# The gate's logits of a mixture-of-experts layer, taken from eight extra columns of the attention's output projection

## The chip, the cores and the metric

The kernel runs on one core of one Trainium2 chip. The metric is device time in microseconds for one execution of the whole kernel; smaller is better. Of several runs the median is given.

## The reference

The input `x` is 2 x 56 x 56 x 256 in fp32. The reference runs two layers over it. Layer 0 is group norm and a 7 x 7 neighbourhood attention with 8 heads, added to `x`. Layer 1 works on the 2 x 3136 tokens of 256 values: a causal linear attention with gates and cumulative sums, and then a feed-forward part with 8 experts of hidden size 512, of which each token takes the two with the largest gate probability. Cut to layer 1:

```
t = t + attn(ln(t), wq, wk, wv, wo, ...)      # ends in  ctxt @ wo.T + bo
z = ln(t)                                     # (t - mean) / sqrt(var + 1e-5)
logits = z @ gate_w + gate_b                  # gate_w: 256 x 8
probs  = softmax(logits)
cw     = probs where among the token's top 2, else 0
t = t + sum over experts e of cw[:, e] * (gelu(z @ W1[e] + b1[e]) @ W2[e] + b2[e])
```

The LayerNorm `z` is needed twice: as the experts' input and for the gate's logits.

## The kernel before, in words

Layer 0 takes the first 447 us and is the same in both kernels. Layer 1 goes over the tokens in 14 steps. A step is 224 tokens of each of the two batch entries, 448 in all, held as four tiles of 112 tokens (`NTI` = 4, `TT` = 112). Three generators and the experts' work make up a step:

- `before_pairs(s)` loads the tokens into `x_acc`, normalizes them to `xn`, transposes `xn` on TensorE (`pt_x`, copied by ScalarE to `xT_a`), and makes q, k, v (`p_qkv`), an auxiliary product (`p_u`), the sums over each head (`p_sum`, from products `pd`) and the scans over the tokens that yield the gate factor `gl` and the coefficients `cf`. It also adds the output bias `bo` to `x_acc`.
- `attention(s)` makes the cumulative sums in pairs of blocks (`p_gt`, `kt`, `vt`, `sc`, `qv`, the running state `zz`, `z` and `zc`, outputs `po`) and then the output projection `p_out`, which is added to `x_acc`.
- `route(s)` stores `x_acc` to the output, normalizes it to `xs`, transposes `xs` (again `pt_x`, copied to `xT_f`), multiplies with the gate's weights (`p_gate`), and goes on with softmax (`pb`), the rank of each expert (`rank`, `taken`), two small matmuls that count tokens by expert (`p_n`), slot numbers (`slot`, `rowi`), and eight indirect DMAs on GpSimd's queue that scatter the rows of `xs` to `xs_d` in DRAM, sorted by expert. `listed` then keeps the list of expert tiles.
- `experts()` goes through 56 tiles of 256 slots. For each it fetches the rows (`xg`) and the expert's weights (`wj`, 1.15 MB) on SP's queue, takes the token numbers out of `xg` (`rows_e`), transposes (`pt_g`), multiplies twice (`p_h`, `hT`, `p_y`), scales (`ye`) and adds the result to the output by an indirect DMA on GpSimd's queue (`out<-ye`).

Both normalizations are one function, `norm_T`: statistics of four tiles (`lst`, `lmv`), standard deviation by a square root on ScalarE (`lrs`), its reciprocal, four `tensor_scalar` operations on VectorE, eight transposes and two copies.

The function `together` interleaves the generators in step s: `attention(s)` leads, with it run `route(s - 1)`, `before_pairs(s + 1)` and expert tiles, each at a given share of the leader's yields (`n_step, n_route = 45, 13`). So the tokens of step s - 1 are normalized for the routing while those of step s + 1 are normalized for the attention. Below that a scheduler sets the final order of the instructions on each engine by its priorities and its own estimates of costs. An engine runs its instructions in that order. The matmuls of all these parts take their PSUM tiles from one pool of six (`l_mm`).

Expert tiles start in step 4, as tokens must have been routed first. After the last step the route of step 13 stands alone with four expert tiles; then follow some sixteen expert tiles until the end.

Layer 1 exists twice in the program, a plain form and a general one, and a value `plain`, worked out from the inputs in layer 0, decides by a branch which one runs. Here it is the plain one.

Of the kernel before, what the change touches and what calls it, by code (L numbers as in the profile page):

```python
# [14 lines left out]
F32 = mybir.dt.float32  # L15
I32 = mybir.dt.int32
U32 = mybir.dt.uint32
AF = mybir.ActivationFunctionType
ALU = mybir.AluOpType
AX = mybir.AxisListType  # L20
PSUM = bass.MemoryType.PSUM
DRAM = bass.MemoryType.DRAM

P = 128
NB = 2
IMG = 56
L = IMG * IMG
C = 256
NG = 2
# [11 lines left out]
TT = 112  # L41
BLK = 448
BT = BLK // NB
NST = L // BT
NTI = BLK // TT
CH = 8
NCH = TT // CH
NE, FF = 8, 512
NF = FF // P
GN_EPS = 1e-5  # L50
LN_EPS = 1e-5
# [6 lines left out]
NX = (2 * NB * L - NE) // SL + NE  # L58
TOK, CWC = C, C + 1
ROW = C + 16  # L60


def sure(s):
# [90 lines left out]
def hybrid_kernel(ctx: ExitStack, tc: tile.TileContext, t: dict, out: bass.AP):  # L154
    nc = tc.nc
    const = ctx.enter_context(tc.tile_pool(name="const", bufs=1))
# [4 lines left out]
    x1_d = dram.tile([NB, IMG, IMG, C], F32, name="x1_d")  # L161
    xs_d = dram.tile([NE * RG + SL, ROW], F32, name="xs_d")
    ident = const.tile([P, P], F32, name="ident")
# [13 lines left out]
    def load(pool, name, shape, src, eng=None, dt=F32):  # L177
        dst = pool.tile(shape, dt, name=name)
        (eng or nc.sync).dma_start(out=dst, in_=src)
        return dst  # L180

    def load_wT(pool, name):
        return load(pool, name, [P, NG, C], t[name].rearrange("(k p) o -> p k o", p=P))


    wq1, wk1, wv1, wo1 = (load_wT(const, f"L1_w{n}T") for n in "qkvo")
    bq1, bk1, bv1 = (load(const, f"b{n}1", [P, NG], t[f"L1_b{n}P"]) for n in "qkv")
    bo1 = load(
        const, "bo1", [TT, C], t["L1_attn_wo_b"].unsqueeze(0).to_broadcast([TT, C])
# [65 lines left out]
    with tc.tile_pool(name="once", bufs=1) as once:  # L255
        s_all = once.tile([P, NG, HD], F32, name="s_all")
        for h in range(4):
            nc.sync.dma_start(
                out=s_all[h * HD : (h + 1) * HD],
                in_=s_row.rearrange("(g h) e -> h g e", g=NG)[h]  # L260
                .unsqueeze(0)
                .to_broadcast([HD, NG, HD]),
            )
        nc.vector.tensor_tensor(s_all, s_all, s_sb, ALU.is_equal)
        nc.vector.tensor_reduce(same, s_all, AX.XY, ALU.min)
    plain = const.tile([1, 1], I32, name="plain")
    ones = const.tile([NB * NH, BT], F32, name="ones")
    nc.gpsimd.memset(ones, 1.0)
# [66 lines left out]
    with (  # L335
# [250 lines left out]
        nc.vector.tensor_reduce(mx[:, 1:2], pf[:, NG + 1, :], AX.X, ALU.min)  # L586
        nc.vector.tensor_copy(plain, mx[:, 1:2])

    flag = nc.values_load(
# [56 lines left out]
    def layer_1(general):  # L648
        with (
# [48 lines left out]
                nc.gpsimd.memset(qh, 0.0)  # L698
                qhs.append(qh)

            def norm_T(x, tag, pool, xn=None):

                st = p2.tile([TT, NTI, 6], F32, tag="lst", name="lst")
                mv = p2.tile([TT, NTI, 2], F32, tag="lmv", name="lmv")
                for i in range(NTI):
                    nc.vector.bn_stats(st[:, i, :], x[:, i, :])  # L706
                    nc.vector.bn_aggr(mv[:, i, :], st[:, i, :])
                rs = p2.tile([TT, NTI], F32, tag="lrs", name="lrs")
                nc.vector.tensor_scalar_add(rs, mv[:, :, 1], LN_EPS)
                nc.scalar.activation(rs, rs, AF.Sqrt)  # L710
                nc.vector.reciprocal(rs, rs)
                xT = pool.tile([P, NG, BLK], F32, tag=tag, name=tag)
                if xn is None:
                    xn = p1.tile([TT, NTI, C], F32, tag="xn", name="xn")
                yield
                for i in range(NTI):
                    nc.vector.tensor_scalar(
                        xn[:, i, :C],
                        x[:, i, :],
                        mv[:, i, 0:1],  # L720
                        rs[:, i : i + 1],
                        ALU.subtract,
                        ALU.mult,
                    )
                for g in range(NG):
                    pt = ps_m.tile([P, NTI, TT], F32, tag="mm", name="pt_x")
                    for i in range(NTI):
                        nc.tensor.transpose(  # L728
                            pt[:, i, :], xn[:, i, g * P : (g + 1) * P], ident[:TT, :TT]
                        )  # L730
                    nc.scalar.copy(xT[:, g, :], pt.rearrange("p i t -> p (i t)"))
                    yield
                return xT

            def before_pairs(s):

                nonlocal m_prev, s_prev, g_prev
                x = p4.tile([TT, NTI, C], F32, tag="x", name="x_acc")
                for b in range(NB):
                    nc.sync.dma_start(  # L740
                        out=x[:, b * 2 : (b + 1) * 2, :],
                        in_=x1_d[b]
                        .rearrange("r c e -> (r c) e")[s * BT : (s + 1) * BT]
                        .rearrange("(i p) e -> p i e", p=TT),
                    )
                yield
                xT = yield from norm_T(x, "xT_a", p1)
                nc.vector.tensor_tensor(
                    x, x, bo1.unsqueeze(1).to_broadcast([TT, NTI, C]), ALU.add
                )  # L750
                q, k, v = (
                    p2.tile([P, NG, BLK], F32, tag=n, name=n) for n in ("q", "k", "v")
# [38 lines left out]
                for g in range(NG):  # L791
                    for b in range(NB):
                        for n in range(4):
                            nc.tensor.matmul(
                                ps[n * HD : n * HD + NHB, :],
                                lhsT=ind[:, g, b, :],
                                rhs=pd[:, n, g, b * BT : (b + 1) * BT],
                                start=at == 0,
                                stop=at == NB * NG - 1,
                            )  # L800
                        at += 1
                row = [NHB, BT]

                def part(n):
# [12 lines left out]
                gl = p2.tile(row, F32, tag="gl", name="gl")  # L817
                nc.vector.tensor_tensor(gl, part(3), rk, ALU.mult)
                yield


                m = p2.tile([NHB, BT + 1], F32, tag="m", name="m")
# [155 lines left out]
            def attention(s):  # L978
                x, q, k, v, gl, cf = ready.pop(s)
                yield from (sums_general if general else sums_plain)(s, q, k, v, gl, cf)  # L980

                for i in range(NTI):
                    ps = ps_m.tile([TT, C], F32, tag="mm", name="p_out")
                    for g in range(NG):
                        nc.tensor.matmul(  # L985
                            ps,
                            lhsT=q[:, g, i * TT : (i + 1) * TT],
                            rhs=wo1[:, g, :],
                            start=g == 0,
                            stop=g == NG - 1,  # L990
                        )
                    nc.vector.tensor_tensor(x[:, i, :], ps, x[:, i, :], ALU.add)
                    yield
                routed[s] = x
                if general:
                    yield from route(s)
# [160 lines left out]
            def route(s):  # L1157
# [3 lines left out]
                for b in range(NB):  # L1161
                    stored.append(
                        nc.gpsimd.dma_start(
                            out=out[b * L + s * BT : b * L + (s + 1) * BT].rearrange(
                                "(i p) e -> p i e", p=TT
                            ),
                            in_=x[:, b * 2 : (b + 1) * 2, :],
                        )
                    )
                xs = p3.tile([TT, NTI, ROW], F32, tag="xs", name="xs")  # L1170
                nc.gpsimd.memset(xs[:, :, CWC + NE :], 0.0)
                xT = yield from norm_T(x, "xT_f", p1, xs)
                pg = ps_m.tile([TT, NTI, NE], F32, tag="mm", name="p_gate")
                for i in range(NTI):
                    for k in range(NG):
                        nc.tensor.matmul(  # L1176
                            pg[:, i, :],
                            lhsT=xT[:, k, i * TT : (i + 1) * TT],
                            rhs=gw[:, k, :],
                            start=k == 0,  # L1180
                            stop=k == NG - 1,
                        )
                pb = p2.tile([TT, NTI, NE], F32, tag="pb", name="pb")
                red = p2.tile([TT, NTI], F32, tag="red", name="red")
                nc.vector.tensor_tensor(
                    pb, pg, gb.unsqueeze(1).to_broadcast([TT, NTI, NE]), ALU.add
                )
                nc.vector.tensor_reduce(red, pb, AX.X, ALU.max)
                nc.vector.tensor_tensor(
                    pb, pb, red.unsqueeze(2).to_broadcast([TT, NTI, NE]), ALU.subtract  # L1190
# [34 lines left out]

                taken = p2.tile([TT, NTI, NE], F32, tag="taken", name="taken")
                nc.vector.tensor_single_scalar(taken, rank, 1.5, ALU.is_lt)
                yield
                pn = ps_m.tile([P, 2, NTI, NE], F32, tag="mm", name="p_n")
                flat = taken.rearrange("p i e -> p (i e)")  # L1230
# [289 lines left out]
            tiles = experts()  # L1520
            per_tile = NF + 1 + SL // P
            n_before = sum(1 for _ in before_pairs(0)) + 1
            n_step, n_route = 45, 13
            for s in range(NST):
                n_tiles = max(0, sure(s - 1) - wait) - max(0, sure(s - 2) - wait)
                begin = n_tiles and sure(s - 2) <= wait
# [92 lines left out]
```

## Time and profile before

| | us |
|---|---|
| median of 3 runs | 1600.95 (1599.42 to 1603.63) |
| the profiled execution, its own time | 1586.77 |
| its span | 1584.9 |
| layer 0, to `plain` | 0 to 447 |
| between the layers, to the first matmul of layer 1 | 447 to 462.6 |
| steps of layer 1 | 463 to 1388 |
| last routing, to the last scatter's issue | 1388 to 1417 |
| last expert tiles | 1417 to 1584.9 |

The span runs from the first to the last instruction. Over it TensorE was busy 1379.4 us (87%), VectorE 921.9 (58%), ScalarE 707.0 (45%) and GpSimd 449.5 (28%), and the mean granted TensorE clock was 0.935. PE is TensorE's matmul, PEld its weight loads, DVE is VectorE, ACT ScalarE, POOL GpSimd, SP SyncE. A fp32 matmul appears as two records in the profile. Durations are taken from the one profiled execution.

### The profile page before, as it was taken

How to read it: one execution, taken by the hardware profiler on the slowest of the kernel's cores; microseconds unless marked ns; L12 is line 12 of the kernel's file. 1: busy time of each engine (PE TensorE's matmuls, PEld its weight loads, DVE VectorE, ACT ScalarE, POOL GpSimd, SP SyncE). 2: the span in 40 equal slices, each digit the busy share in tenths (PEclk: the TensorE clock that was granted, in tenths of full speed). 3: DMA queues.
4: the chain of work that ended last, by engine and by line, in shares of the span. 5: the costliest groups of instructions: out<-in, count | busy, mean ns of one | idle time of the engine just before them, and what ended most of it. 6: DMA issues, size and time to landing. Idle time of an engine off the chain costs nothing. (4 is left out here: it accounts for less than half of the span.)

```text
span 1584.9 us, 28462 instructions
## 1 busy us (share of the span) xinstructions
PE 1379.4 (87%) x10672; PEld 1008.6 (64%) x10672; DVE 921.9 (58%) x2731; ACT 707.0 (45%) x1261; POOL 449.5 (28%) x496
## 2 busy tenths in 40 slices
PE   0789999999957779878999998999999899879996
PEld 0357667677834445555766766676776667667885
DVE  3546566656646786785756757576766757441221
ACT  0333343444424344335664655565555546243342
POOL 2113233333320021112233231313223232343443
PEclk9989999999969688679999999999999999889998
DMA  7445554455520010114434443434443443459884
GB/s 222 140 130 167 161 171 151 138 164 156 165 70 0 24 48 26 36 36 173 121 116 116 114 119 110 125 104 119 110 113 105 130 112 93 120 162 264 234 231 90
DMA packets 110769, 197.66 MB, mean 125 GB/s; under 512 B 17666, under 2 KB 92274, under 8 KB 103444
## 3 DMA queue, kind: packets, MB, share of 16 engines
q1 hardware_dynamic: 74596, 135.60, 26.8%
q0 software_dynamic: 32560, 54.55, 14.9%
q10 hardware_dynamic: 3456, 5.51, 1.1%
q8 instruction: 88, 1.44, 0.4%
q14 instruction: 69, 0.57, 0.1%
HBM read 138.85 MB, written 56.73 MB: 123 GB/s over the span
## 5 line engine op out<-in xcount | busy, mean ns | idle before, releaser
L1457 POOL DMA_INDIRECT out<-ye,rows_e x112 | 176.8, 1579 | 429.7 <-DVE ye L1454 199.4
L1409 PE MATMUL p_h<-xT_g,wj 128*128 128x256 f32 x896 | 233.8, 395 | 4.9 <-DVE ye L1454 4.9
L1447 PE MATMUL p_y<-wj,hT 128*128 128x256 f32 x896 | 217.0, 389 | 7.6 <-issue 4.0
L1409 PEld LDWEIGHTS p_h<-xT_g,wj 128*128 128x128 f32 x896 | 168.1, 196 | 47.9 <-issue 19.8
L1447 PEld LDWEIGHTS p_y<-wj,hT 128*128 128x128 f32 x896 | 169.9, 194 | 44.1 <-issue 18.2
L512 ACT ACTIVATE ex<-ex 98x1024 f32<-98x1024 f32 x98 | 103.9, 1060 | 202.5 <-DVE ex L506 193.5
L1267 POOL DMA_INDIRECT xs_d<-xs,rowi x112 | 106.7, 953 | 194.5 <-DVE pos L1322 73.8
L506 DVE TENSOR_TENSOR ex<-sc,bias 98x1024 f32<-98x1024 f32 x98 | 119.5, 1220 | 47.8 <-PE sc L497 42.5
L1416 ACT ACTIVATE hT<-p_h,wj 128x256 f32<-128x256 f32 x224 | 103.9, 471 | 87.7 <-PE p_h L1409 79.5
L521 PE MATMUL po<-vw,ex 98*64 98x33 f32 x3136 | 116.6, 227 | 8.3 <-DMA vw<-v_d 8.2
L1454 DVE SCALAR_TENSOR_TENSOR ye<-p_y,cws,ye 128x256 f32<-128x256 f32 x112 | 53.5, 478 | 116.1 <-PE p_y L1447 115.9
L521 PEld LDWEIGHTS po<-vw,ex 98*64 98x64 f32 x3136 | 104.5, 141 | 24.7 <-DMA vw<-v_d 10.1
L1441 ACT ACTIVATE ye<-wj,cws 128x256 f32<-128x256 f32 x112 | 54.4, 502 | 143.7 <-DVE own_e L1428 114.4
L497 PEld LDWEIGHTS sc<-qb,kc 64*98 64x98 f32 x1568 | 92.5, 166 | 40.6 <-issue 26.4
L497 PE MATMUL sc<-qb,kc 64*98 64x128 f32 x1568 | 114.4, 285 | 1.3 <-DVE ex L506 1.3
L926 PE MATMUL sc<-qh,v 128*112 128x448 f32 x224 | 109.4, 575 | 0.0
L934 DVE TENSOR_TENSOR qv<-sc,upto 112x448 f32<-112x448 f32 x112 | 68.9, 616 | 57.8 <-PE sc L926 55.9
L324 POOL TENSOR_TENSOR xo<-xo,xq 128x256 f32<-128x256 f32 x49 | 35.5, 725 | 157.6 <-DVE xo L318 149.0
L1424 DVE CAST rows_e<-xg 128x2 int32<-128x2 f32 x56 | 9.3, 166 | 116.6 <-DMA xg<-xs_d 116.5
L985 PE MATMUL p_out<-L_woT,q 128*112 128x256 f32 x224 | 64.3, 417 | 9.1 <-DVE q L975 9.1
L1416 ACT ACT_TABLE_LOAD x44 | 56.5, 1283 | 26.6 <-PE p_h L1409 26.0
L446 ACT ACTIVATE kc<-pk,bk 128x112 f32<-128x112 f32 x196 | 50.6, 371 | 37.4 <-PE pk L415 37.4
(229 smaller groups left out, 2468.2 us busy)
## 6 DMA issues: line engine op xcount, KB each, us to landing
wj<-in_we SPq DMA_DIRECT2D x56, 1154.0 KB
vw<-v_d SPq DMA_DIRECT2D x196, 101.1 KB
xg<-xs_d SPq DMA_DIRECT2D x56, 272.0 KB
v_d<-values POOLq DMA_DIRECT2D x28, 231.0 KB
xq<-in_x SPq DMA_DIRECT2D x98, 64.0 KB
q_d<-evq POOLq DMA_DIRECT2D x28, 224.0 KB
qb<-q_d SPq DMA_DIRECT2D x56, 112.0 KB
x_d<-xo POOLq DMA_DIRECT2D x98, 64.0 KB
```

Of the source, the lines that this page charges most:

```text
L497: nc.tensor.matmul(sc[:KN, p, b, k], lhsT=keys(i, j, k, b, rows, g), rhs=qb[rows, g, :, b, j * QN : (j + 1) * QN], start=True, stop=True,)
L506: nc.vector.tensor_tensor(ex[:KN], sc[:KN].rearrange("n p b k h q -> n p b (k h q)"), tables[kind][:KN, g].unsqueeze(2).to_broadcast(wide) ...
L512: nc.scalar.activation(ex[:KN], ex[:KN], AF.Exp)
L521: nc.tensor.matmul(po[b * QN : (b + 1) * QN, hh, :], lhsT=ex[:KN, p, b, k, h, :], rhs=vw[:KN, b, k, hh * (HD + 1) : (hh + 1) * (HD + 1)], ...
L926: nc.tensor.matmul(sc, lhsT=vg[:, i * TT : (i + 1) * TT], rhs=qh[:, :, i * TT : (i + 1) * TT], start=True, stop=True,)
L934: nc.vector.tensor_tensor(qv, sc, upto.unsqueeze(1).to_broadcast([TT, 4, TT]), ALU.mult)
L985: nc.tensor.matmul(ps, lhsT=q[:, g, i * TT : (i + 1) * TT], rhs=wo1[:, g, :], start=g == 0, stop=g == NG - 1,)
L1267: d = nc.gpsimd.indirect_dma_start(out=xs_d[:, :], out_offset=bass.IndirectOffsetOnAxis(ap=rowi[:, c, i : i + 1].bitcast(U32), axis=0), in ...
L1409: nc.tensor.matmul(ph, lhsT=w1[:, k, f * P : (f + 1) * P], rhs=xT[:, k, :], start=k == 0, stop=k == NG - 1,)
L1416: nc.scalar.activation(hT[:, f, :], ph, AF.Gelu, bias=b1[:, f : f + 1])
L1447: nc.tensor.matmul(py, lhsT=hT[:, f, u * P : (u + 1) * P], rhs=w2[:, f, :], start=f == 0, stop=f == NF - 1,)
L1457: d = nc.gpsimd.indirect_dma_start(out=out[:, :], out_offset=bass.IndirectOffsetOnAxis(ap=rows[:, u : u + 1].bitcast(U32), axis=0), in_=y, ...
```

## The change

The logits are linear in the normalized tokens, so they can be made from the token before the normalization: with x2 the sum of the token and the attention's output, logits = (x2 @ gate_w - mean(x2) * gsum) / sd(x2) + gate_b, where `gsum` is the sum of the gate's weights over the 256 inputs. And x2 @ gate_w is the sum of three parts: ctxt @ (wo.T @ gate_w), the input's own part, and bo @ gate_w (`bog`).

- The output projection's weight `wo1` becomes 264 columns wide; the eight more columns hold wo.T @ gate_w. `p_out` yields them with the rest, and they are added to eight more columns of `x_acc`.
- `before_pairs` gets the gate's products `p_gate`, now from `xT_a`, after `p_sum`. From them, the standard deviation `lsd`, the mean and `bog`, four small VectorE operations make the input's part and put it into the extra columns.
- `route` has neither transposes nor copies `xT_f` nor gate products. It takes the extra columns, subtracts mean times `gsum` (`mg`), multiplies by the reciprocal and adds `gb`. The normalization to `xs` remains, as the experts need it, and is written after `taken`.
- `norm_T` is split into `moments`, `norm` and `mean_gates`.
- A new function `gate_sums`, which runs once between the layers, makes `gsum`, `bog` and the eight columns: one small DMA, four transposes and eight small matmuls, with copies between them.
- `n_route` goes from 13 to 11, as `route` has two yields fewer.

By engine, the plain branch and what is ahead of it have 112 transposes fewer on TensorE (the four transposes and eight matmuls of `gate_sums` come on top), 98 small operations more and ten of `gate_sums` on VectorE, 28 copies and 4 table loads fewer on ScalarE, the same instructions on GpSimd and one DMA more on SP. On GpSimd's queue the order of the scatters and the `out<-ye` additions is different: a few `out<-ye` now stand between the eight scatters of a step.

```diff
+CX = C + NE
...
-    wq1, wk1, wv1, wo1 = (load_wT(const, f"L1_w{n}T") for n in "qkvo")
+    wq1, wk1, wv1 = (load_wT(const, f"L1_w{n}T") for n in "qkv")
+
+    wo1 = const.tile([P, NG, CX], F32, name="wo1")
+    nc.sync.dma_start(out=wo1[:, :, :C], in_=t["L1_woT"].rearrange("(k p) o -> p k o", p=P))
...
+    def gate_sums(pool, psum):
+        bo_c = load(pool, "bo_c", [P, NG, 1], t["L1_attn_wo_b"].rearrange("(k p o) -> p k o", p=P, o=1))
+        wide = pool.tile([P, NG, 2, TT], F32, name="wide")
+        nc.vector.tensor_copy(wide[:, :, 0, :], bo_c.to_broadcast([P, NG, TT]))
+        nc.vector.memset(wide[:, :, 1, :], 1.0)
+        for n, o in ((1, gsum), (0, bog)):
+            ps = psum.tile([TT, NE], F32, tag="pj", name="p_gs")
+            for k in range(NG):
+                nc.tensor.matmul(
+                    ps, lhsT=wide[:, k, n, :], rhs=gw[:, k, :], start=k == 0, stop=k == NG - 1
+                )
+            nc.vector.tensor_copy(o, ps)
+        for g in range(NG):
+            wT = pool.tile([P, NG, P], F32, name=f"wT{g}")
+            for k in range(NG):
+                pt = psum.tile([P, P], F32, tag="pj", name="p_wT")
+                nc.tensor.transpose(pt, wo1[:, g, k * P : (k + 1) * P], ident)
+                nc.vector.tensor_copy(wT[:, k, :], pt)
+            ps = psum.tile([P, NE], F32, tag="pj", name="p_wg")
+            for k in range(NG):
+                nc.tensor.matmul(
+                    ps, lhsT=wT[:, k, :], rhs=gw[:, k, :], start=k == 0, stop=k == NG - 1
+                )
+            nc.vector.tensor_copy(wo1[:, g, C:], ps)
...
-            def norm_T(x, tag, pool, xn=None):
+            def moments(x):
...
+                sd = p2.tile([TT, NTI], F32, tag="lsd", name="lsd")
+                nc.vector.tensor_scalar_add(sd, mv[:, :, 1], LN_EPS)
+                nc.scalar.activation(sd, sd, AF.Sqrt)
...
+            def mean_gates(mv):
+
+                mg = p2.tile(gates, F32, tag="mg", name="mg")
+                nc.vector.tensor_tensor(
+                    mg,
+                    gsum.unsqueeze(1).to_broadcast(gates),
+                    mv[:, :, 0:1].to_broadcast(gates),
+                    ALU.mult,
+                )
+                return mg
...
+                pg = ps_m.tile(gates, F32, tag="mm", name="p_gate")
+                for i in range(NTI):
+                    for kk in range(NG):
+                        nc.tensor.matmul(
+                            pg[:, i, :],
+                            lhsT=xT[:, kk, i * TT : (i + 1) * TT],
+                            rhs=gw[:, kk, :],
+                            start=kk == 0,
+                            stop=kk == NG - 1,
+                        )
...
+                mg = mean_gates(mv)
+                xg = x[:, :, C:]
+                nc.vector.tensor_tensor(
+                    xg, pg, sd.unsqueeze(2).to_broadcast(gates), ALU.mult
+                )
+                nc.vector.tensor_add(mg, mg, bog.unsqueeze(1).to_broadcast(gates))
+                nc.vector.tensor_add(xg, xg, mg)
...
-                    ps = ps_m.tile([TT, C], F32, tag="mm", name="p_out")
+                    ps = ps_m.tile([TT, CX], F32, tag="mm", name="p_out")
...
-                xT = yield from norm_T(x, "xT_f", p1, xs)
-                pg = ps_m.tile([TT, NTI, NE], F32, tag="mm", name="p_gate")
...
+                mv, _, rs = moments(x)
+                yield
...
-                nc.vector.tensor_tensor(
-                    pb, pg, gb.unsqueeze(1).to_broadcast([TT, NTI, NE]), ALU.add
-                )
+                nc.vector.tensor_sub(pb, x[:, :, C:], mean_gates(mv))
+                nc.vector.tensor_tensor(pb, pb, rs.unsqueeze(2).to_broadcast(gates), ALU.mult)
+                nc.vector.tensor_add(pb, pb, gb.unsqueeze(1).to_broadcast(gates))
...
                 nc.vector.tensor_single_scalar(taken, rank, 1.5, ALU.is_lt)
+                norm(x, mv, rs, xs)
...
-            n_step, n_route = 45, 13
+            n_step, n_route = 45, 11
```

## The prediction

> **What bounds the kernel now.** I read the slices of the page first, to see where the change falls. A slice is 39.6 us; layer 1 begins in slice 12, at 455 us.
>
> ```profile
> PE   0789999999957779878999998999999899879996
> DVE  3546566656646786785756757576766757441221
> PEclk9989999999969688679999999999999999889998
> ```
>
> From slice 18 on TensorE is at 8 or 9 tenths in nearly every slice and VectorE at 4 to 7: layer 1 is TensorE-bound there. Slices 12 to 17 are different: TensorE at 5 to 9, VectorE up to 8, and a clock that sinks to 0.6 and 0.8. Those are the first steps, without expert tiles to fill the holes. Next came the table of windows, because a share over the span hides this. Its columns are the stretch, its length, then busy time of PE, PEld, DVE, ACT and POOL, clock, DMA share and GB/s.
>
> ```profile
> 463.00:600.00 137.00, 107.43 (x576) 66.42 (x576) 94.18 (x265) 57.68 (x99) 10.52 (x13) 0.81 0.07 21
> 600.00:700.00 100.00, 84.37 (x465) 52.28 (x463) 78.50 (x259) 41.58 (x70) 18.37 (x22) 0.81 0.11 34
> 700.00:1300.00 600.00, 559.43 (x3180) 403.63 (x3180) 391.04 (x1363) 339.48 (x571) 170.35 (x152) 0.97 0.41 116
> ```
>
> In 700 to 1300, TensorE is busy 93%. A microsecond of its work is worth a microsecond, unless a wait takes its place. So the third view is what TensorE waits for (us in total, times, longest):
>
> ```profile
> PE pt_x L728 <- DVE xs L717: 39.8, 13, 6.1
> PE pt_x L728 <- DVE xn L717: 17.1, 2, 16.5
> PE p_sum L794 <- DVE pd L787: 9.5, 5, 2.8
> PE p_n L1231 <- DVE taken L1227: 2.4, 1, 2.4
> ```
>
> The longest wait of layer 1 is the one the change removes: the transposes of the routing's normalized tokens `xs`. Its first three cost 16.0 us, nine in steady steps about 2.4 each, the last 2.0. The last view is the timeline around one of them:
>
> ```profile
> 912.91 1.38 DVE L717 TENSOR_SCALAR xs<-x_acc,lmv,lrs 112x256 f32<-112x256 f32 x4
> 913.38 0.32 PE L728 MATMUL pt_x<-ident,xs 112*128 112x112 f32 x1 [2.23 <-DVE xs L717]
> 914.21 1.38 DVE L717 TENSOR_SCALAR xn<-x_acc,lmv,lrs 112x256 f32<-112x256 f32 x4
> ...
> 985.05 0.17 DVE L1424 CAST rows_e<-xg 128x2 int32<-128x2 f32 x1 [1.62 <-DMA xg<-xs_d]
> 985.12 1.37 DVE L717 TENSOR_SCALAR xn<-x_acc,lmv,lrs 112x256 f32<-112x256 f32 x4
> ```
>
> The reader is to see that `xn`, the attention's normalized input of a later step, comes on VectorE right behind `xs`. Its transposes wait for nothing today only because those of `xs` waited already. In the odd step (lower pair) `xn` also stands behind a `rows_e` that waits for a DMA.
>
> [...] `pb<-pb,red` 112x32 has a median of 191 ns. [...] The order is borne out by `xn` above, which starts only behind `rows_e`.
>
> **The change part by part.**
>
> *TensorE.* 112 transposes of `xs` (8 a step, 14 steps) go. A record lasts 257 to 451 ns, but groups of four start 0.40 us apart (985.85 and 986.25), so one is worth 0.10 us: −11 us in all. The output projection takes 264 columns for 256: 224 records, 64.3 us busy, by 8/256: +2.0 us. The 112 gate products are issued as before, but in `before_pairs` after `p_sum`: 0 as work; the `po` and `zz` behind them start 1.5 us later (all 16 records of a step took 1.66 at 1395.47), and the routing's later ones as much earlier. Pure work: **−9 us**, 0.65 a step.
>
> *ScalarE.* 28 copies `xT_f` of 0.53 us and 4 table loads of 1.28 us: −20 us. It is busy 340 of 600 us; worth nothing by itself.
>
> *VectorE.* Seven small operations a step more: 98 by 0.19 = +18.6 us, and 56 `x_acc` adds of 0.42 us wider by 3%: +0.7. In 700 to 1300 it is busy 391 of 600, so the sum is hidden; what counts is their place. In the changed order `mg`, `pb` and two of their like stand ahead of `xs` and `xn`.
>
> *The start.* `gate_sums` runs between the layers. Its bias DMA can start when `plain` is made (446.96). [...] Then wide copies 0.3, two sums with their copies 1.0, and for each of two halves two transposes, two products and three VectorE copies, each waiting for the other engine, 1.3: 453.1. The branch takes another 2.1 (SP resumes at 451.28, POOL's last store is issued at 449.15), so layer 1 begins at 455.2, not 451.3: +4. Bounds: 0, if the DMA lands sooner and the branch overlaps, and +6. The gate products stand in the chain of the first step, and small operations with them: +1. Sum **+5**.
>
> *Steps 1 to 3.* The 16.0 us of stalls stand here, at a clock of 0.81. Three times 0.65 of pure work at that clock is −2.4; the stall on `xs` turns into one on `xn`, which is at most 2 us earlier or later. I take −3, bounds −12 and +5.
>
> *Even steady steps* (as 902 to 960). I replay the changed order with the durations above. TensorE now does `p_vt` (0.6) before the stall and arrives at 911.8. VectorE has at 912.6 the reciprocal, then four `xs`, `kt` (0.69) and four small operations in between, so the first `xn` is done at 913.9: a stall of 2.1 in place of 2.23. With the transposes gone TensorE is 0.9 ahead. Next late is the second `zz`, whose PSUM waits for the `z` adds, which stand behind the rank operations: 1.3. Then `p_n`, which is now placed right behind it, while `taken` is not ready: 0.9. Before, `p_n` came at 930.80, 3.5 us after `taken` (927.33). So 1.3 us is lost. The stall on `pd` (9.5 over five even steps) comes from `rows_e`, which waited 6.8 us for a chain of scatter and fetch; scatters start some 5 us earlier, and I give back 1.3 of its 1.9. Sum 0, bounds −2 and +2 a step.
>
> *Odd steady steps* (as 969 to 1000). The fetch `xg` is tied to freed buffers, so `rows_e` still ends at 985.2; in the changed order it stands ahead of `pb`, `xs` and `xn` together. What stood before it, four `xs`, now partly follows, with small operations: the first `xn` is done at 986.8. TensorE, transposes saved, is 1.6 behind where it was. Queued behind its wait are all matmuls of the expert tile. +1.6, bounds −3 and +3.5.
>
> *Five pairs of steady steps:* **+8**, bounds −25 and +27.
>
> *The tail.* After the last `x_acc` (1387.9) the path runs LayerNorm, transposes, gate products (1397.2), softmax, rank, `taken` (1403.4), slots, eight scatters (1407.3 to 1416.9), fetches. Without transposes and gate products `taken` is 4.6 us earlier. But in POOL's changed order one `out<-ye` stands between the second scatter and the other six, and it needs an expert tile that ends about 1409: scatters end about 1418 by my replay. Bounds −4 and +1.5; **−1**.
>
> *Sum:* +5 −3 +8 −1 = **+9 us**. It is made against the profiled execution (span 1584.9, 1586.8 in all), which is 14.2 us, 0.9%, below the median of the runs shown, 1600.95. On that scale the forecast is 1601 + 9 = **1610 us**. What a measurement of this kernel tells from no change is about 0.3%, 4.8 us.
>
> **The rivals.**
>
> *A. The stall only changes its name and grows* (above): +9, from 0 to +22. For it: `xn` right behind `xs` on VectorE, and strict order. Chance 0.45.
>
> *B. The stall goes.* TensorE keeps the 9 us, and of the 21.8 us of steady stalls and 16.0 of early ones a good half goes too, because with less on ScalarE and a shorter chain VectorE catches up: −9 − 19 + 5 = −23, 1578; from −8 to −35. For it: 93% busy TensorE, and the replay is of two steps out of ten. Against it: `xn` on VectorE. It decides from the point where `xn` is ready less than 1 us after TensorE comes to it. Chance 0.33.
>
> *C. Work saved and start cancel:* the other stalls stay as they are, −9 + 5 = −4; 1597. Chance 0.12.
>
> *D. VectorE becomes the bound* in the first 240 us of layer 1 and around 904 to 916, where it has no gap: four early steps by 1.5 us plus ten by 1.3 plus the start: +24, 1625. Against it: VectorE idle a third of the steady stretch. Chance 0.10.
>
> That the change does not do what it says is excluded for the transposes: the changed order of TensorE has none of `xs`.
>
> **How the numbers follow.** A is the likeliest: 1610; its own range is 1601 to 1623. Faster by over 0.3%: 0.30 of B and 0.05 of C, 0.35. Within: 0.11 of A, 0.03 of B, 0.05 of C: 0.19. Slower: 0.34 of A, 0.02 of C, 0.10 of D: 0.46. The range leaves out the fast third of B and the slow half of D, and what A has beyond its own: 1580 to 1625.
>
> **What would show it.** Right: waits of `pt_x` on `xn` of about 2 us in steady steps, waits of `zz` on `z` and of `p_n` on `taken`; the first matmul of layer 1 near 467 instead of 462.6; 61 us or more a step. Wrong: waits of `pt_x` that sum to under 20 us between 463 and 1450 and no new ones; or TensorE's stalls moved to the routing's reciprocal `lrs`. The last scatter before 1414 would say that the tail is mis-sized, and the first `pt_x` before 464 that the start costs nothing.

## The result and the profile after

In the first comparison the changed kernel took 1622.44 us (median of 4 runs, 1614.21 to 1624.26) against 1600.53 (4 runs): a ratio of 1.0124, 95% interval 1.0086 to 1.0161. A later one gave 1.0151 (1.0028 to 1.0275). It is slower, by some 20 us in both. The ratios in this document compare only the faster executions of the two kernels, so a ratio need not be that of the means beside it. The forecast was +9, in a range that ended at +24. At equal mean clock the change costs 7 to 10 us (below). The profiles show 7.5 us of that in the start of layer 1; what the rest of layer 1 gains or loses is smaller than what profiles of one kernel differ by. What is left of the 20 us goes with TensorE's clock, in the profiles for the most part that of layer 0, whose instructions are the same in both kernels.

The slices of the page after, to be laid beside those of before:

```profile
PE   0689999999984877887988999898999999889996
DVE  3456466656335578766558494665759466552121
PEclk9989899999557978898999999999899999989998
```

The clock is at 5 in slices 10 and 11, counted from 0. That is layer 0, which ends (`plain`) at 475.4 us here and at 446.8 in the profile of before. The windows of 400 to 450 us, after and before (length, then PE, PEld, DVE, ACT, POOL busy, clock, DMA share, GB/s):

```profile
400.00:450.00 50.00, 50.00 (x637) 45.63 (x636) 20.56 (x28) 13.91 (x14) 12.99 (x21) 0.50 0.40 116
```
```profile
400.00:450.00 50.00, 41.74 (x890) 37.10 (x888) 27.10 (x44) 18.15 (x18) 18.65 (x30) 0.93 0.47 141
```

At half the clock TensorE is busy all the time and gets 637 matmul records done instead of 890. Since the kernel before fell into this too when it was run again (below), layer 1 is compared by itself. Its stages by the timelines, in us, between marks that both kernels have: `plain`; the first `p_gt` of steps 0, 4 and 13; the last addition of `p_out` to `x_acc`; the last scatter's issue; the end of the span. Two profiles of each kernel, and one more of each with an edit (`xq`, below) that moves only loads of layer 0:

| kernel | layer 0 ends | start | steps 0-4 | steps 4-13 | 13 to last `x_acc` | routing, scatters | rest | layer 1 |
|---|---|---|---|---|---|---|---|---|
| before | 446.8 | 40.9 | 205.9 | 636.2 | 57.7 | 28.5 | 168.9 | 1138.1 |
| before, again | 482.1 | 41.2 | 205.9 | 632.2 | 57.4 | 26.8 | 170.6 | 1134.0 |
| after | 475.4 | 49.6 | 206.8 | 644.3 | 49.3 | 30.6 | 164.0 | 1144.7 |
| after, again | 475.3 | 47.5 | 203.5 | 643.5 | 49.0 | 30.2 | 165.2 | 1138.8 |
| before, `xq` | 494.1 | 42.1 | 205.9 | 642.8 | 57.0 | 26.7 | 170.6 | 1145.2 |
| after, `xq` | 487.9 | 49.7 | 206.5 | 641.2 | 51.9 | 30.8 | 165.5 | 1145.6 |

In the first two pairs layer 1 is 5.7 us longer on the mean: start +7.5, steps to the last `x_acc` +0.5, routing and rest −2.4 (the parts are rounded). In the third pair it is 0.4 us longer. The three profiles of before differ by 11 us among themselves, nearly all of it in steps 4 to 13, so only the start is clear of that spread: it is 6.3 to 8.7 us longer in every pair.

What TensorE waited for in steps 4 to 13, after (732 to 1376 us; us in total, times, longest):

```profile
PE p_u L838 <- DVE kt L980: 13.2, 4, 4.5
PE pt_x L798 <- DVE xn L756: 7.8, 5, 3.4
PE pt_x L798 <- DVE pb L1256: 7.7, 4, 2.6
PE zz L1022 <- ACT vt L994: 7.6, 4, 1.9
PE p_n L1299 <- DVE taken L1294: 5.0, 8, 2.1
```

The same stretch before (694 to 1330) begins with these and has neither `p_u`, `p_n` nor `zz` on `vt`:

```profile
PE pt_x L728 <- DVE xs L717: 25.2, 9, 5.0
PE p_sum L794 <- DVE pd L787: 9.1, 4, 2.8
```

All waits together were 45.9 us and are 53.1 (45.3 and 51.7 in the second pair). The stall on `xs` is gone. In its place `pt_x` waits 15.5 us for `xn` or for an operation of `pb` that stands among the `xn`, and four further names have come up.

### The profile page after: what moved, and what is told of

The parts are those of the page before. It is cut to its first block, busy times and chain, and to the rows that moved or that the text cites. A ratio compares the mean times of both kernels' runs of the same rounds, so it can differ in the third digit from the quotient of the medians.

```text
span 1620.1 us, 28346 instructions
## 1 busy us (share of the span) xinstructions
PE 1407.1 (87%) x10580; PEld 1021.8 (63%) x10580; DVE 921.0 (57%) x2839; ACT 684.9 (42%) x1229; POOL 449.8 (28%) x496
## 3 DMA queue, kind: packets, MB, share of 16 engines
q8 instruction: 86, 1.41, 0.4%
## 5 line engine op out<-in xcount | busy, mean ns | idle before, releaser
L1477 PE MATMUL p_h<-xT_g,wj 128*128 128x256 f32 x896 | 229.9, 392 | 5.1 <-ACT xT_g L1467 3.8
L1515 PE MATMUL p_y<-wj,hT 128*128 128x256 f32 x896 | 217.1, 387 | 10.3 <-ACT hT L1484 4.1
L554 PE MATMUL po<-vw,ex 98*64 98x33 f32 x3136 | 130.8, 242 | 5.1 <-DMA vw<-v_d 5.0
L554 PEld LDWEIGHTS po<-vw,ex 98*64 98x64 f32 x3136 | 118.9, 159 | 23.1 <-DMA vw<-v_d 6.3
L530 PEld LDWEIGHTS sc<-qb,kc 64*98 64x98 f32 x1568 | 106.4, 187 | 40.1 <-issue 26.8
L530 PE MATMUL sc<-qb,kc 64*98 64x128 f32 x1568 | 130.6, 313 | 0.0
L1002 PE MATMUL sc<-qh,v 128*112 128x448 f32 x224 | 113.4, 598 | 0.0
L1239 POOL DMA_DIRECT2D out<-x_acc x28 | 20.4, 730 | 197.0 <-DVE x_acc L1068 137.3
L1061 PE MATMUL p_out<-wo,q 128*112 128x264 f32 x224 | 64.6, 415 | 9.0 <-DVE q L1051 9.0
L974 ACT COPY qh<-q 32x448 f32<-32x448 f32 x112 | 62.9, 561 | 9.8 <-PE sc L1002 8.0
```

The lines of the kernel that those rows point to most:

```text
L530: nc.tensor.matmul(sc[:KN, p, b, k], lhsT=keys(i, j, k, b, rows, g), rhs=qb[rows, g, :, b, j * QN : (j + 1) * QN], start=True, stop=True,)
L554: nc.tensor.matmul(po[b * QN : (b + 1) * QN, hh, :], lhsT=ex[:KN, p, b, k, h, :], rhs=vw[:KN, b, k, hh * (HD + 1) : (hh + 1) * (HD + 1)], ...
L1002: nc.tensor.matmul(sc, lhsT=vg[:, i * TT : (i + 1) * TT], rhs=qh[:, :, i * TT : (i + 1) * TT], start=True, stop=True,)
L1061: nc.tensor.matmul(ps, lhsT=q[:, g, i * TT : (i + 1) * TT], rhs=wo1[:, g, :], start=g == 0, stop=g == NG - 1,)
L1477: nc.tensor.matmul(ph, lhsT=w1[:, k, f * P : (f + 1) * P], rhs=xT[:, k, :], start=k == 0, stop=k == NG - 1,)
L1515: nc.tensor.matmul(py, lhsT=hT[:, f, u * P : (u + 1) * P], rhs=w2[:, f, :], start=f == 0, stop=f == NF - 1,)
```

## The experiments

Times between executions of one kernel spread over 40 us, and they go with the mean clock. On the 67 runs of the kernel before that belong to the first four experiments, time falls by 12.0 us for each 0.01 of mean clock. "At 0.920" below is the mean over a kernel's runs after each is moved along that slope to a mean clock of 0.920; ± is twice the standard error. On the runs of before that belong to the other two groups the slope is 10.4 and 12.9. This also levels what clock layer 1 itself had, so the stage times of the profiles stand beside it.

| kernel | runs | mean us | mean clock | at 0.920 | ratio to before |
|---|---|---|---|---|---|
| before (chip of the next four) | 67 | 1607.8 | 0.919 | 1607.0 ± 0.7 | |
| again | 22 | 1610.2 | 0.917 | 1606.7 ± 1.2 | 0.998 (0.994 to 1.003) |
| early_sums | 14 | 1607.4 | 0.921 | 1608.9 ± 1.5 | 0.994 (0.988 to 1.000) |
| late_norm | 22 | 1608.4 | 0.922 | 1610.4 ± 1.4 | 1.005 (0.998 to 1.011) |
| few_small | 22 | 1607.5 | 0.920 | 1607.9 ± 1.7 | 1.000 (0.996 to 1.004) |
| before (chip of the next four) | 11 | 1613.4 | 0.916 | 1609.1 ± 2.1 | |
| xq_before | 6 | 1633.9 | 0.908 | 1618.9 ± 3.5 | 1.016 (1.010 to 1.021) |
| xq_after | 6 | 1635.6 | 0.912 | 1626.2 ± 1.0 | 1.017 (1.011 to 1.023) |
| xq_both | 6 | 1619.3 | 0.917 | 1615.9 ± 1.7 | none given |
| xq_both_rows | 6 | 1582.2 | 0.922 | 1585.0 ± 2.2 | 0.984 (0.978 to 0.989) |
| before (chip of the next four) | 27 | 1595.2 | 0.926 | 1603.0 ± 1.4 | |
| after_again | 6 | 1614.8 | 0.918 | 1612.8 ± 3.9 | 1.015 (1.003 to 1.028) |
| rows_before | 6 | 1560.3 | 0.933 | 1575.9 ± 2.6 | 0.978 (0.962 to 0.994) |
| rows_after | 22 | 1581.1 | 0.926 | 1588.4 ± 1.0 | 0.993 (0.987 to 0.998) |
| rows_both | 6 | 1556.8 | 0.932 | 1571.6 ± 1.8 | 0.978 (0.968 to 0.988) |

**The kernel before once more** (no edit).

> The kernel before, unchanged, profiled once more. In the two profiled executions so far, `plain` is made at 446.8 us before and at 475.4 after, with TensorE's clock at 0.50 from 398 us on in the second, though layer 0's instructions are the same. Theory 1 (the drop of the clock in layer 0 is chance, it comes after a short wait of TensorE for a transfer, and both kernels have it in some executions): the median is again near 1600, 13 us above the first profiled execution, so in most executions layer 0 ends later than at 446.8, between 450 and 475, with a clock of 0.50 in a part of 390 to 446. Theory 2 (the change causes it): `plain` at 446 to 449 again, clock above 0.9 in 400 to 446.

Theory 1 holds, with more delay than expected (450 to 475): layer 0 ends at 482.1 us, with a clock of 0.50 from 397 on; the 67 runs of before range from 1580 to 1625 us. The first profile of before, against which the prediction made its sum, had one of the lucky layers 0. The times of a kernel that differ by up to 45 us from run to run need a stage table, or the clock beside the time.

**`gate_sums` ahead of layer 0.**

```diff
+    with (
+        tc.tile_pool(name="gs", bufs=1) as p1,
+        tc.tile_pool(name="gs_p", bufs=2, space=PSUM) as ps_p,
+    ):
+        gate_sums(p1, ps_p)
+
     l0 = ExitStack()
```

(The same block between the layers is taken out.)

> The changed kernel with `gate_sums` written ahead of layer 0, where TensorE has nothing to do until 47 us. The first transposes of layer 1 came 15.8 us after `plain` before and 23.1 after the change. If `gate_sums` between the layers is what delays the start: 15.8 to 17 us after `plain` here, and a time 5 to 8 us below the changed kernel's. If the delay is the slower clock or the loads after the branch instead: 21 us or more, and no gain. Theory 2 on layer 0's clock (a cause that lies in `gate_sums`' place, as it changes what the scheduler puts at the end of layer 0): the clock in 390 to 446 is above 0.9 here.

The timelines at the first transposes of layer 1, after (`plain` at 475.44) and here (`plain` at 475.89):

```profile
487.99 0.06 DVE L708 MEMSET m_first<- 16x1 f32 x1 [5.31 <-DMA upto<-in_upto]
...
498.56 1.93 PE L798 MATMUL pt_x<-ident,xn 112*128 112x112 f32 x8 [16.08 <-DVE xn L756]
```
```profile
483.98 0.06 DVE L709 MEMSET m_first<- 16x1 f32 x1 [7.95 <-DMA repb<-in_L_attn_kv_norm_scale]
...
491.83 1.93 PE L799 MATMUL pt_x<-ident,xn 112*128 112x112 f32 x8 [16.66 <-DVE xn L757]
```

VectorE's first instruction of layer 1 comes 8.1 us after `plain` instead of 12.6, and the transposes 15.9 us instead of 23.1; before it was 8.2 and 15.8. So the whole delay is `gate_sums` between the layers: 4.4 us for itself, and 2.7 more as the loads of `x_acc` land later behind it (the first by 2.0 us, the last by 2.8, beyond the 4.4). The start is 42.5 us. Layer 1 as a whole gained nothing in this profile (1141.3 us): steps 0 to 4 took 210.6. By the times at 0.920 the expected 5 to 8 us are there: 1.9 above before on its chip, where the changed kernel is 7 to 10 above before on others. Layer 0 fell to a clock of 0.50 here as well, so `gate_sums`' place isn't what makes that.

**The normalizations to `xs` behind `taken`.**

```diff
-                nc.vector.tensor_single_scalar(taken, rank, 1.5, ALU.is_lt)
-                norm(x, mv, rs, xs)
+                chosen = nc.vector.tensor_single_scalar(taken, rank, 1.5, ALU.is_lt)
+                for d in norm(x, mv, rs, xs):
+                    follow(d, [chosen], "the attention's tokens first")
```

(`norm` returns its four instructions.)

> The changed kernel with the four normalizations to `xs` ordered behind `taken` on VectorE; they then stand in the gap in which VectorE waits for `p_n`, and `xn` has only small operations ahead of it. Theory of the prediction (the stall of `pt_x` only moved from `xs` to `xn`, since `xn` stands behind `xs`): waits of `pt_x` on VectorE are under 10 us in steps 1 to 13, and those of `p_n` on `taken` (13.6 us) shrink; 8 to 20 us faster than the changed kernel. Rival (the steps are bound by other waits, on `zz`, `vt` and the fetches): within 5 us of the changed kernel, the waits appear behind other names.

Between the two. `p_n` on `taken` falls from 12.7 to 7.1 us, and `pt_x` on `xn` and `pb` from 15.8 to 13.6, which misses the expected 10. Steps 4 to 13 take 639.7 us for 644, the tail gives it back (13 to the last `x_acc` is 55.7 for 49); layer 1 is 1146.0, no gain in this profile. `p_u` still waits 14.2 us for `kt` here. The experiment with `rows_e`, below, takes that away.

**Few small operations.** Left out are the terms of mean and deviation in the logits.

```diff
-                mg = mean_gates(mv)
-                xg = x[:, :, C:]
-                nc.vector.tensor_tensor(
-                    xg, pg, sd.unsqueeze(2).to_broadcast(gates), ALU.mult
-                )
-                nc.vector.tensor_add(mg, mg, bog.unsqueeze(1).to_broadcast(gates))
-                nc.vector.tensor_add(xg, xg, mg)
+                nc.vector.tensor_copy(x[:, :, C:], pg)
...
-                nc.vector.tensor_sub(pb, x[:, :, C:], mean_gates(mv))
-                nc.vector.tensor_tensor(pb, pb, rs.unsqueeze(2).to_broadcast(gates), ALU.mult)
-                nc.vector.tensor_add(pb, pb, gb.unsqueeze(1).to_broadcast(gates))
+                nc.vector.tensor_tensor(
+                    pb, x[:, :, C:], gb.unsqueeze(1).to_broadcast(gates), ALU.add
+                )
```

> The changed kernel without the mean's and the deviation's part of the logits: `before_pairs` has one copy of `p_gate` in place of four small operations, `route` one addition in place of four; 84 of the 98 additional VectorE operations are left out. The logits lack these terms, so tokens go to other experts; the number of instructions of the rest is the same. If VectorE's added operations matter (they stand ahead of `xs` and `xn`): 84 x 0.19 = 16 us of VectorE work go, of which what lies on TensorE's way is won, 6 to 16 us. If they are hidden beside TensorE: within 4 us of the changed kernel.

Inconclusive. By stages there is no gain: layer 1 takes 1143.4 us, steps 4 to 13 take 642.9. By the times at 0.920 it is 1 us above before on its chip, where the changed kernel itself is 7 to 10 above before on others. The 84 operations that were left out, of the additional 98, cost something between nothing and some 9 us.

**Layer 0's loads `xq` on ScalarE's queue**, in the kernels before and after, and with the two edits above together.

```diff
-            nc.sync.dma_start(
+            nc.scalar.dma_start(
                 out=xq[b * QN : (b + 1) * QN, :],
```

> The kernel before with the 98 small loads `xq` of layer 0 issued from ScalarE's queue instead of SP's. In six profiled executions TensorE waited once or more for a load `vw` near 395 us (0.45 to 2.3 us) and the clock fell to 0.50 there or near 440 and stayed there to the end of layer 0; SP issues six loads a tile of layer 0, some 4.4 us of issues in a tile of 4.2 us. Theory (SP's issues are what makes `vw` late, the wait makes the clock fall): without `xq` on SP there are no such waits, the clock is above 0.9 from 390 to 440, `plain` is made at 440 to 447, and the times lie within 8 us of one another near 1580. Rival (the clock falls on its own account, or `vw` waits for its buffer and not for SP): times spread over 30 us as before.

The times contradict the theory's forecast, and only a part of it was tested. TensorE's waits for `vw` near 395 us are gone, and the clock falls nevertheless:

```profile
350.00:400.00 50.00, 48.44 (x758) 37.25 (x760) 34.33 (x55) 20.93 (x36) 20.14 (x32) 1.00 0.49 146
400.00:450.00 50.00, 50.00 (x634) 45.56 (x632) 19.76 (x26) 14.30 (x14) 11.15 (x18) 0.50 0.42 127
450.00:490.00 40.00, 40.00 (x514) 36.53 (x515) 16.00 (x22) 11.06 (x11) 10.09 (x17) 0.50 0.24 73
```

But the edit brought another wait just ahead of the fall. ScalarE's queue now issues the loads, and TensorE waits 1.41 us for `ex` from ScalarE:

```profile
398.95 1.39 PE L521 MATMUL po<-vw,ex 98*64 98x33 f32 x32 [1.41 <-ACT ex L512]
```

So SP's issues aren't needed for the fall; whether a short wait of TensorE is stays open. Layer 0 ends at 494.1 us, later than ever without the edit. Of the twelve executions profiled for the experiments, eleven fell to 0.50 between 390 and 415 us and one (few_small) between 435 and 440.

> The changed kernel with the same edit of layer 0. If layer 0 is quiet now, this is the change without the disturbance: by the stage table of the profiles (start +8.7, steps and tail about 0) 7 to 11 us slower than the kernel before with that edit. If the change had caused the slower layer 0: 20 us and more slower, with `plain` again near 475.

1635.6 against 1633.9 us on the mean, at 0.920 +7.3 ± 3.6; the start is 49.7 us for 42.1. That is the expected 7 to 11. Layer 0 ends at 487.9, earlier than with the edit on before, so the change doesn't lengthen it here. In these two profiles layer 1 differs by 0.4 us only (1145.6 and 1145.2): steps 4 to 13 and the tail make up for the start.

> The changed kernel with that edit, `gate_sums` ahead of layer 0, and the normalizations to `xs` behind `taken`. If the start is what the change costs (first `p_gt` 49.6 us after `plain` against 40.9, 42.5 with early sums) and the late normalization gives some of its 7 us in the steps: 5 to 12 us faster than the changed kernel with the edit, that is 3 slower to 4 faster than before with it. If the gain in the steps is lost again in the tail, as the first profile of late normalization hints (steps 844 for 851, tail 241 for 233): 6 us faster, no more.

At 0.920 it is 10.3 us below `xq_after`; layer 1 takes 1131.0 us for 1145.6. The start has 42.6 for 49.7, steps 4 to 13 have 632.0 for 641.2. The second is not shown to be the late normalization's: with TensorE's order of these steps the same, the profile of late_norm has 639.7.

**`rows_e` on GpSimd.**

```diff
-                nc.vector.tensor_copy(rows, xg[:, :, TOK : TOK + 1].rearrange("p u o -> p (u o)"))
+                nc.gpsimd.tensor_copy(rows, xg[:, :, TOK : TOK + 1].rearrange("p u o -> p (u o)"))
```

> As the last one, and the casts `rows_e` on GpSimd instead of VectorE, ahead of the `out<-ye` that read them. In the changed kernel VectorE waits 140 us for `xg` in these casts, up to 11.2 each, and in odd steps `q`, `kt` and `pd` stand behind one, so that TensorE waits for `kt` (`p_u`, 13.2 us in four steps). Theory (the fetch behind the scatters, through VectorE's strict order, is what replaced the stall on `xs`): the waits of `p_u` on `kt` go, and the time falls by 8 to 20 us. Rival (`own_e`, which reads `xg` too, waits in its place, or the casts hold GpSimd's scatters up): within 4 us, with the wait on VectorE under the name `own_e`.

Layer 1 falls from 1131.0 to 1096.8 us, more than expected, and `p_u` no longer waits for `kt` at all. What VectorE waited for in these casts in steps 4 to 13, before and after the change:

```profile
DVE rows_e L1424 <- DMA xg<-xs_d: 70.2, 23, 6.8
```
```profile
DVE rows_e L1492 <- DMA xg<-xs_d: 117.9, 22, 11.2
```

The timeline of the changed kernel shows what one of them does; the load of `xg` is issued at 987.19:

```profile
990.00 0.17 DVE L1492 CAST rows_e<-xg 128x2 int32<-128x2 f32 x1 [7.81 <-DMA xg<-xs_d]
990.08 0.62 DVE L1051 TENSOR_TENSOR q<-po,rb 128x448 f32<-128x448 f32 x1
990.61 0.68 DVE L980 TENSOR_TENSOR kt<-p_kt,glT 112x512 f32<-112x512 f32 x1
...
991.35 0.98 PE L838 MATMUL p_u<-v,wbd 128*128 128x448 f32 x1 [2.93 <-DVE kt L980]
```

A cast of 0.17 us holds VectorE for 7.81 us. Behind it stand `q` and `kt`, and behind `kt` TensorE. At 0.920 the edit takes 30.9 us off here.

The same edit by itself on before, on after, and on after with early sums and late normalization:

> The changed kernel once more, in as many rounds as the kernel before had when it was run again (1607.8 us on the mean of 67 runs, 1601.0 on the line through time and clock at a clock of 0.925). In two profiles of each, layer 1 took 1138.1 and 1134.0 before, 1144.7 and 1145.6 after (the second with layer 0's `xq` loads moved). If the first comparison's +22 us was for the most part the chance of layer 0's clock: 4 to 11 us slower than before, on the line at 0.925 some 1605 to 1612. If the change makes layer 0's slow clock more frequent: 15 us and more slower, `plain` later than 470 in most.

+9.8 ± 4.1 us at 0.920, in the raw means +19.6. The rest of the raw difference is clock: 0.918 for 0.926. The raw difference, and `plain` at 475.3, would also fit the theory that the change makes layer 0's slow clock more frequent; but the kernel before reached 482.1 when it was run again.

> The kernel before with the casts `rows_e` on GpSimd. With the change, early sums and late normalization the same edit took layer 1 from 1131.0 to 1096.8 us. If the wait for `xg` in VectorE's queue was as much a bound before the change (102 us of waiting): layer 1 at 1105 to 1115 instead of 1134 to 1138, 20 to 30 us faster. If it is the changed kernel alone that suffers from it: within 5 us of before.

Layer 1 takes 1093.2 us for 1136 (the mean of two), the time at 0.920 is 27 us lower. Of the 43 us, 11.5 are in steps 0 to 4, where no expert tile and so no cast runs: the order of instructions is the same there, and the clock was 0.877 for 0.815. The rest, and the 27 us, show that the wait for `xg` was as much a bound before the change; the waits of `pd` behind it (`p_sum`, 9.1 us) were its visible part.

> The changed kernel with the casts `rows_e` on GpSimd. If the saved transposes (9 us of TensorE) were lost to VectorE's waits for `xg`: layer 1 is as long as that of before with the same edit or up to 8 us shorter, start of +8.7 us included. If they were lost elsewhere (`zz`, `vt`, `p_n`): 5 to 10 us longer than that, as without the edit.

Neither the equality nor the small excess: 12.5 us above `rows_before` at 0.920, and 1115.1 us for 1093.2 in layer 1. Start 49.2 for 41.4, steps 0 to 4 take 207.8 for 194.4 (the quick ones of `rows_before`), steps 4 to 13 take 617.3 for 618.5. The theory that VectorE's waits for `xg` had eaten the saved transposes falls by the last of these, which should have shown the gain. From step 6 on two steps take 133.6 us for 134.5 on the mean: with the transposes gone and the casts out of the way, next to nothing is won.

> The changed kernel with early sums, late normalization and `rows_e` on GpSimd, layer 0 as it was: the version that the runs point to. Layer 1 at 1097 us as with the `xq` edit, so some 35 to 40 us under the kernel before at the same clock of layer 0: near 1570 on the mean, and below before with `rows_e` on GpSimd by 8 to 18 us if the change is worth its transposes once its start and VectorE's order are mended.

At 0.920 it is 31.4 us under before and 16.8 under `rows_after`; layer 1 takes 1089.1 us. The time is 0.978 (0.968 to 0.988) of before. Against `rows_before` it is 4.3 ± 3.2 us faster at 0.920, not the expected 8 to 18. Waits of TensorE in steps 4 to 13, `rows_both`:

```profile
PE zz L1025 <- ACT vt L997: 7.6, 4, 1.9
PE pt_x L801 <- DVE xn L757: 6.3, 8, 2.1
PE zz L1025 <- DVE lmv L747: 4.3, 1, 4.3
PE p_h L1481 <- ACT xT_g L1471: 2.9, 1, 2.9
PE zz L1025 <- DVE z L1034: 2.7, 5, 1.1
PE p_n L1303 <- DVE taken L1297: 2.1, 1, 2.1
```

and `rows_before`:

```profile
PE pt_x L728 <- DVE xs L717: 26.2, 8, 7.5
PE pt_g L1395 <- DMA xg<-xs_d: 6.1, 1, 6.1
```

The 26.2 us on `xs` have become 6.3 on `xn`, and steps 4 to 13 take 603.3 us for 618.5. Here is the gain that the change can give. The late normalization and the early start together are worth 18 to 26 us of layer 1 once `rows_e` is off VectorE: 1115.1 in `rows_after`, 1089.1 here and 1096.8 in xq_both_rows, whose instructions of layer 1 are the same in the same order. 6 of that are in the start and 14 in steps 4 to 13 (603.3 and 602.7); the 7 in steps 0 to 4 don't come again (201.0 and 208.1 for 207.8). From step 6 on two steps take 130.7 and 130.6 us, for 133.6 in `rows_after` and 134.5 in `rows_before`.

## Why the prediction was right or wrong

**The direction and the mechanism were right, the sizes only in part**: the stall on `xs` moved to `xn`, which stands among the `xs` on VectorE. In steps 4 to 13, 25.2 us became 15.5 of `pt_x`, 13.2 of `zz` (all releasers) and 5.0 of `p_n`; a further 13.2 of `p_u` came up behind `rows_e`. `rows_both` shows the cause as far as the order goes: with `xs` out of `xn`'s way the steps are 14 us shorter than in `rows_after`. With `rows_e` still on VectorE the same order won only 2 to 5 us there (late_norm). The sum was forecast as +9. It came out as +5.7 for layer 1 in the first two pairs of profiles and +0.4 in the third, and as +7.3 and +9.8 in the times at equal clock. Of the signs named, `pt_x` waits 1.7 us a time for `xn` or `pb` (2 expected), and `zz` on `z` and `p_n` on `taken` are there; "61 us or more a step" tells nothing, as steps 4 to 13 took 70.7 us each before the change.

**The start**, +5 forecast, is +8.7 in the first profile and +7.5 on the mean. The barrier was right (+4.4 for +4). The time for its DMA in that sum was the author's estimate, which no trace of before shows; the profile of after has about as much, 2.1 us (issued at 475.71, read at 477.80). What the step left out is that the loads of `x_acc` land 2.0 to 2.8 us later behind it.

**Steps 1 to 3**, −3 forecast: −0.8 on the mean of two profiles (205.2 for 205.9). The 11 us of stalls on `xs` went, and `p_n` (7.7) and `zz` (7.6 on VectorE's operations) took their place. That the mean clock was 0.86 for 0.815 there played a part that isn't separated.

**The steady steps**, +8 forecast: steps 4 to 13 are +9.7 (643.9 for 634.2) in the first two pairs, where the clock was 0.952 for 0.963 and 0.971. At like clocks nothing is left of it: −1.6 in the `xq` pair (0.957 and 0.958) and −1.2 between `rows_after` and `rows_before`, which have the casts elsewhere (0.970 and 0.967). The longer waits (+7.2 and +6.4 us, +3 in the `xq` pair) thus offset the saved work, forecast as 0.65 a step, more or less, and the +8 is not confirmed; whether the change itself lowers the clock there stays open. The replay's stalls came, though not where it put them. In a timeline of after, TensorE's wait for the first `xn` is 1.38 us at 957.37, an odd step of the table. The replay of odd steps had `rows_e` ahead of `xn`; what was late there was `kt`, behind a `rows_e` half a step later, and `p_u` with it. The 1.3 us that even steps were to get back from `pd` did come back (9.1 to 0). That +9.7 agrees with +8 is luck.

**After step 13** nothing was forecast up to the last `x_acc`; it is 8.4 us shorter (49.2 for 57.6). Step 12's routing has no transposes (0.8) and no gate products (1.7) there; the clock is 1.00 instead of 0.91 in it. With both at 1.00, `rows_after` is 2.5 us shorter there than `rows_before` (45.1 for 47.6), which is those two; so I put the remaining 6 us (8.4 less 2.5), an estimate, down to the clock.

**The tail** was right in its size: from the last `x_acc` to the end −2.4 us, −1 forecast. `taken` comes 5.1 us earlier (4.6 forecast), and the last scatter 2.7 later, since three `out<-ye` hold GpSimd: two ahead of the scatters (1.68 and 1.56 us) and one between the second and the third, whose issues are 5.99 us apart where those of the next are 1.24.

**The step that was missing** is layer 0. The sum was made against one profiled execution and its 14 us under the median were taken as a scale factor. They were for the most part layer 0 at full clock: it ended at 446.8 us, where eight of the nine later profiles without the `xq` edit have 473 to 482 (the ninth, few_small, has 442.3). So the 0.3% (4.8 us) that the prediction took as the limit of what a measurement tells was too small: 67 runs of before spread over 45 us. Two comparisons put a further 10 us or so on the changed kernel by the clock; that 1622 still fell into the range is owed to its width. Kernels with the same layer 0 and most of the change (early_sums, late_norm, few_small) had the clock of before on the same chip (0.920 to 0.922 for 0.919). So it reads as chance, but six and four runs of the changed kernel don't settle whether it changes the odds.

**Rivals.** B, TensorE keeps its 9 us and the stalls go, did not happen. Its condition, `xn` ready in time, could be made nearly so in `rows_both`, together with the early start; against `rows_before` that is 4.3 us faster and not 23. C, the work saved and the start cancel, has against it that the waits changed their names and that the times at equal clock are +7.3 and +9.8 for −4; the layer 1 of the profiles alone (+0.4 in the `xq` pair) would not exclude it. D, VectorE as the bound by its added operations, isn't shown: few_small wins nothing by stages.

## What to carry to other kernels

When a stall is taken away, look at the next instruction in that engine's order and at what it needs: here the next operand came from the same queue, right behind the one removed, and 25.2 us of waits for `xs` became 15.5 for `xn` and `pb`. A cast of 0.17 us that waited for a transfer cost VectorE the whole wait, 7.81 us in the timeline above; here it was better placed on the queue that uses its result (24 to 31 us at equal clock, in three pairs of kernels). And where the time varies by more than the effect, compare stages between marks that both kernels have, in several profiles and with the clock of each stage beside it: one and the same stage differed by 11 us.

## What the runs showed of the hardware

In twelve of the fourteen profiles TensorE's clock fell to 0.50 between 390 and 415 us and stayed there for the 77 to 95 us that were left of layer 0, while the profile shows it busy without a gap. In the profile of after these are matmuls of 98 x 64 by 33 and 64 x 98 by 128: 50.00 of 50 us busy between 400 and 450, and the clock at 0.50 throughout. In all fourteen the fall comes within 5 us of the beginning of a wait of TensorE of 0.4 to 2.5 us, in xq_before the 1.41 us shown above. But not every such wait brings one: before, TensorE had four waits of 0.5 to 1.6 us between 393 and 424 and kept the full clock to 443; in few_small it had three of 0.45 to 0.81 us and kept it to 437. What decides it stays open.
